# VectorE's order in the last phase: left to the scheduler, or written in the source with a pair's update spread over the next pair's evictions

## The chip, the cores and the metric

The kernel runs on one core of a Trainium2 chip. A core has five engines with queues of their own: TensorE (matmul), VectorE, ScalarE, GpSimd, and SyncE, which here issues DMAs. An instruction is issued in the order of its engine's queue, once the semaphores that it waits for have been counted up by the instructions it depends on. The metric is the device time of one launch in microseconds, lower is better.

## The reference

Two layers on 128 graphs of 128 nodes with 256 features, each wrapped in a residual and a layer norm. The first is a gated graph convolution. The second, which the change touches, joins a convolution branch and a message branch in a gated recurrent unit:

```python
# layer 0
norm = jnp.power(jnp.sum(adj, axis=-1) + 1e-06, -0.5)[..., None]
f_hom = jnp.einsum('bnm,bmd->bnd', adj, (x @ theta) * norm) * norm
gate = jax.nn.sigmoid(x @ W_t + b_t)
x = _layernorm(x + jax.nn.elu(gate * f_hom + (1.0 - gate) * (x @ W_h)))
# layer 1
h = jax.nn.relu(_bn(_conv1d(xc, conv1_w, 0), ...))
h = _bn(_conv1d(h, conv2_w, 8), ...)
x_conv = jnp.transpose(jax.nn.relu(h + xc), (0, 2, 1))
s = x @ w_se.T + b_se
A = jnp.exp(-dist(s)) * adj
x_nmp = jnp.einsum('bnm,bmd->bnd', A, jax.nn.relu(x @ w_msg.T + b_msg))
gi = jnp.concatenate([x_conv, x_nmp], axis=-1) @ w_ih.T + b_ih
gh = x @ w_hh.T + b_hh
r = jax.nn.sigmoid(gi_r + gh_r)
z = jax.nn.sigmoid(gi_z + gh_z)
nn_ = jnp.tanh(gi_n + r * gh_n)
x = _layernorm(x + (1.0 - z) * nn_ + z * x)
```

All of it is float32.

## The kernel before

The kernel has three phases. The first (to about 662 us) runs layer 0, `conv1` and the analysis of the 17-tap convolution into a frequency basis, two graphs at a time. The second multiplies in that basis, one pair of frequencies per step (L789 to L822), to about 839 us. The last phase, from 839 us to the end, takes the 128 graphs in 32 groups g of four, `NG` = 32, and each group in two pairs pr of two graphs.

In the last phase a group passes through these functions:

- `l1_own` (L945): masks the coordinates (`own`, VectorE L958), once per four groups after a transpose on TensorE and a copy on ScalarE (`turned`).
- `l1_kernel` (L963), for two groups at once: distance matmuls into `acc`, exponential on ScalarE (L976), times the adjacency on VectorE (`AT`, L980).
- `l1_project` (L921): sums of the node features on GpSimd (`sh`), message matmuls into two PSUM banks, evicted by VectorE with the bias (`msg`, L937), relu on ScalarE (L941). Groups 2 and 3 (`EARLY`) have their messages from an earlier phase.
- `l1_synth` (L890), for two groups at once: matmuls back from the frequency basis into `acc`, four evictions on VectorE (L914, with scale and residual), each with a relu on ScalarE (L917, `xcT`), then sums on GpSimd (`sc`).
- `l1_gather` (L983): messages times `AT` on TensorE, copied by ScalarE (`nmpT`, L993), then four sums on VectorE (`sm`, L1003 to L1006).
- `l1_gru` (L1041), per pair: the gate matmuls in seven products (Strassen's scheme with Winograd's sums). Each product is three float32 matmuls (of `sh`, `sc`, `sm` or the plain tiles, with the weights or the factors `t_h`, `t_c`, `t_m` that `l1_factors` makes once at the start, L844 to L847) into one PSUM bank. VectorE evicts each bank while adding it to a running sum: L1069 (product 0), L1072 (1), L1073 (5), L1074 (6), L1075 (4), L1096 (3), L1097 (2). GpSimd adds two more (L1094, L1095).
- `l1_update` (L1010), per pair: the elementwise end of the recurrent unit and the layer norm. It is a generator. Its steps are tanh of both gates on ScalarE (L1015), then on VectorE L1019, L1021 (with ScalarE's tanh L1022 behind), L1025, L1027, L1029, L1031, the statistics (L308, L309) with GpSimd's rstd (L192, L193), `nb` on VectorE (L316), the normalisation on ScalarE (L318) and the store of the result (L1038, SyncE's queue).

PSUM in this phase: four banks that go round (`psC`, taken through `bankc`), for messages, `nmp`, transposes and products; and one tile of four banks (`acc`), shared by the synthesis and the distance matmuls. `o` and `y` have two buffers each, `u1` to `p5` one.

The order. The code is issued through a scheduler that sorts each engine's instructions by priorities and its own view of times. Inside `tc.manual_schedule(engines=...)` the engines named keep the order of the source. Before, that held in the last phase for TensorE alone (L1104), and for TensorE, VectorE and ScalarE in the very last pair (L1133), whose update is written out by halves (L1076 to L1093). Everywhere else in the last phase VectorE's order was the scheduler's: a pair's update ran through at once in the source (L1098), and the scheduler put its steps between the next pair's evictions.

Of the kernel before, what the change touches and what calls it, by code (L numbers as in the profile page):

```python
# [18 lines left out]
G = 4  # L19
# [15 lines left out]
def gnn_layers_kernel(ctx: ExitStack, tc: tile.TileContext, a: dict, out: bass.AP):  # L35
# [80 lines left out]
    st = {}  # L116
# [206 lines left out]
    def nodes(q):  # L323
        return slice(q * P, (q + 1) * P)
# [246 lines left out]
    E = mybir.EngineType  # L571
# [218 lines left out]
    with tc.manual_schedule(engines={E.Activation, E.Pool}):  # L790
        for k in range(M // 2):
# [3 lines left out]
            y = yb.tile([P, 2, D], F32, tag="y", name=f"yb_{k}")  # L795
# [62 lines left out]
    def load_x1(g):  # L858
# [10 lines left out]
            s["x1"], x1_d[2 * g : 2 * g + 2].rearrange("r j n e -> n (r j) e")  # L869
        )  # L870

    sy = {}

    def load_y(d):
# [15 lines left out]
    def l1_synth(d):  # L890
        four = acc.tile([P, 4, 512], F32, tag="acc", name=f"conv2_ps_{d}")
        pcs = {}
        for e in range(2):
            for c in range(NC):
                pc = pcs[e, c] = four[:, NC * e + c, :]
                for q in range(G):
                    nc.tensor.matmul(  # L897
                        pc[:, nodes(q)], lhsT=sy[2 * d + e][0][:, q, c * P : (c + 1) * P], rhs=S,
                        start=(q == 0), stop=False, skip_group_check=True,
                    )  # L900
        for e in range(2):
            for c in range(NC):
                k = slice(32 * (NC * e + c), 32 * (NC * e + c) + 32)
                nc.tensor.matmul(  # L904
                    pcs[e, c], lhsT=sy[2 * d + e][1][k, :],
                    rhs=SLb[k].rearrange("p q n -> p (q n)"),
                    start=False, stop=True, skip_group_check=True,
                )
        for e in range(2):
            s = st[2 * d + e]  # L910
            s["xcT"] = ck.tile([P, NC, G * P], F32, tag="xcT", bufs=3, name=f"xcT_{2 * d + e}")
            for c in range(NC):
                dst = s["xcT"][:, c, :]
                nc.vector.scalar_tensor_tensor(  # L914
                    dst, pcs[e, c], scale2[:, c : c + 1], s["x1T"][:, c, :], ALU.mult, ALU.add
                )
                nc.scalar.activation(dst, dst, AF.Relu, bias=shift2[:, c : c + 1])  # L917
            l1_sums(2 * d + e, "c", s["xcT"], nc.gpsimd)


# [42 lines left out]
    def l1_kernel(*groups):  # L963

        pd = acc.tile([P, G, 512], F32, tag="acc", name=f"dist_ps_{groups[0]}")
        for i, g in enumerate(groups):
            turned, own = st[g]["turned"], st[g]["own"]
            for q in range(G):
                k = slice(q * P // G, (q + 1) * P // G)
                nc.tensor.matmul(  # L970
                    pd[:, q, i * P : (i + 1) * P], lhsT=turned[k, 0, :], rhs=own[k, :],
                    start=True, stop=True, skip_group_check=True,
                )
        for i, g in enumerate(groups):
            AT = st[g]["AT"] = ck.tile([P, G * P], F32, tag="AT", bufs=3, name=f"AT_{g}")
            nc.scalar.activation(  # L976
                AT.rearrange("p (q n) -> p q n", q=G), pd[:, :, i * P : (i + 1) * P],
                AF.Exp, scale=-1.0,
            )
            nc.vector.tensor_mul(AT, AT, st[g]["adjT"].rearrange("p q n -> p (q n)"))  # L980


    def l1_gather(g):  # L983
        s = st[g]
        nmpT = ck.tile([P, NC, G * P], F32, tag="nmpT", name=f"nmpT_{g}")
        for c in range(NC):
            pn = bankc(f"nmp_ps_{g}_{c}")
            for q in range(G):
                nc.tensor.matmul(  # L989
                    pn[:, nodes(q)], lhsT=s["msg"][:, q, c * P : (c + 1) * P],  # L990
                    rhs=s["AT"][:, nodes(q)], start=True, stop=True,
                )
            nc.scalar.activation(nmpT[:, c, :], pn, AF.Copy)  # L993
        l1_sums(g, "m", nmpT, nc.vector)


    def l1_sums(g, kind, src, engine):

        v = src.rearrange("p c (r j n) -> p c r j n", r=G // 2, j=2)
        a11, a12, a21, a22 = (v[:, c, :, j, :] for j in range(2) for c in range(NC))  # L1000
        t = ck.tile([P, 4, G // 2, P], F32, tag=f"s{kind}", name=f"s{kind}_{g}")
        s1, s2, s3, s4 = (t[:, i] for i in range(4))
        engine.tensor_tensor(s1, a21, a22, ALU.add)  # L1003
        engine.tensor_tensor(s2, s1, a11, ALU.subtract)
        engine.tensor_tensor(s3, a11, a21, ALU.subtract)
        engine.tensor_tensor(s4, a12, s2, ALU.subtract)  # L1006
        st[g][f"f{kind}"] = (a11, a12, s4, a22, s1, s2, s3)
# [33 lines left out]
    def l1_gru(g, pr, between=()):  # L1041

        s = st[g]
        y = ck.tile([P, 2, D], F32, tag="y", name=f"y_{g}_{pr}")
        add, sub = ALU.add, ALU.subtract

        made = iter(range(7))
        between = dict(between)

        def product(i):  # L1050
            k = next(made)
            if k in between:
                between[k]()
            pg = bankc(f"g_ps_{g}_{pr}_{i}")
            for k, (kind, lo) in enumerate((("h", 0), ("c", P), ("m", P))):
                nc.tensor.matmul(  # L1056
                    pg[:, lo : lo + 3 * P], lhsT=s[f"f{kind}"][i][:, pr, :], rhs=factors[kind][i],
                    start=(k == 0), stop=(k == 2), skip_group_check=True,
                )
            return pg  # L1060

        def sums(name):
            return ck.tile([P, 2 * D], F32, tag=name, bufs=1, name=f"{name}_{g}_{pr}")


        o = ck.tile([P, 2, 2, 2 * D], F32, tag="o", name=f"o_{g}_{pr}")
        u1, u2, u3, u4, p5 = (sums(q) for q in ("u1", "u2", "u3", "u4", "p5"))
        v = nc.vector
        v.tensor_tensor(u1, product(0), bias[:, 0, :], add)  # L1069
        final = g == NG - 1 and pr + 1 == G // 2  # L1070
        if not final:
            v.tensor_tensor(o[:, 0, 0, :], product(1), u1, add)  # L1072
        v.tensor_tensor(u2, product(5), u1, add)  # L1073
        v.tensor_tensor(u3, product(6), u2, add)  # L1074
        v.tensor_tensor(p5, product(4), bias[:, 1, :], add)  # L1075
        if final:  # L1076

            v.tensor_tensor(o[:, 1, 1, :], u3, p5, add)
            v.tensor_tensor(o[:, 1, 0, :], u3, product(3), sub)
            steps = [l1_update(g, pr, o[:, 1:2], y[:, 1:2], 1, 2)]  # L1080
            next(steps[0])
            v.tensor_tensor(u4, u2, p5, add)
            next(steps[0])
            next(steps[0])
            v.tensor_tensor(o[:, 0, 0, :], product(1), u1, add)
            next(steps[0])
            v.tensor_tensor(o[:, 0, 1, :], product(2), u4, add)
            steps.append(l1_update(g, pr, o[:, 0:1], y[:, 0:1], 0, 1))
            next(steps[1])
            for k in range(9):  # L1090
                for step in steps if k < 7 else reversed(steps):
                    next(step, None)
            return  # L1093
        nc.gpsimd.tensor_tensor(u4, u2, p5, add)  # L1094
        nc.gpsimd.tensor_tensor(o[:, 1, 1, :], u3, p5, add)  # L1095
        v.tensor_tensor(o[:, 1, 0, :], u3, product(3), sub)  # L1096
        v.tensor_tensor(o[:, 0, 1, :], product(2), u4, add)  # L1097
        for _ in l1_update(g, pr, o, y, 0, 2):  # L1098
            pass
        if pr + 1 == G // 2:  # L1100
            del st[g]

    ND = NG // 2
    with tc.manual_schedule(engines={mybir.EngineType.PE}):  # L1104
        load_c(0)
        load_c(1)
        load_y(0)
        for g in range(2):
            load_x1(g)
            l1_own(g)  # L1110
        l1_project(0)
        l1_kernel(0, 1)
        l1_project(1)
        l1_factors()
        l1_synth(0)
        for g in range(NG):
            d = g // 2
            if g + 2 < NG:
                load_c(g + 2)
                if g % 2 == 0:  # L1120
                    load_y(d + 1)
                load_x1(g + 2)
                l1_own(g + 2)
            l1_gather(g)
            if 2 <= g + 1 < NG:
                l1_project(g + 1)
            l1_gru(g, 0)
            if g % 2 == 1 and d + 1 < ND:
                l1_synth(d + 1)
            if g + 1 < NG:  # L1130

                l1_gru(g, 1, {4: lambda: l1_kernel(g + 1, g + 2)} if g % 2 == 1 else {})
    with tc.manual_schedule(engines={E.PE, E.DVE, E.Activation}):  # L1133
        l1_gru(NG - 1, 1)
    cctx.close()
# [41 lines left out]
```

## Time and profile before

| | us |
|---|---|
| median of three runs | 1980.65 (1980.35 to 1981.75) |
| the profiled execution | 1981.01 |
| its span, first to last instruction | 1979.2 |
| TensorE matmul busy | 1948.1 (98%) |
| VectorE busy | 1452.3 (73%) |
| ScalarE busy | 743.7 (38%) |
| GpSimd busy | 704.4 (36%) |

The costliest groups by line in the last phase are the products (L1056), with 44% of the chain that ended last. VectorE's groups in this phase, between 870 and 1950 us (busy us and mean ns of one, then idle time just before them and what ended it):

```profile
L1019 DVE SCALAR_TENSOR_TENSOR o<-o 128x512 f32<-128x512 f32 x63 | 52.8, 838 | 69.2 <-ACT o L1015 69.2
...
L1097 DVE TENSOR_TENSOR o<-g_ps,u 128x512 f32<-128x512 f32 x62 | 42.9, 692 | 81.9 <-PE g_ps L1056 81.9
...
L1005 DVE TENSOR_TENSOR sm<-nmpT 128x256 f32<-128x256 f32 x31 | 28.7, 927 | 0.0
L1003 DVE TENSOR_TENSOR sm<-nmpT 128x256 f32<-128x256 f32 x31 | 20.8, 671 | 0.0
...
L316 DVE SCALAR_TENSOR_TENSOR nb_b<-mv_b,rstd_b 128x2 f32<-128x2 f32 x62 | 17.8, 287 | 57.2 <-POOL rstd_b L193 57.2
```

How to read it: a timeline row is start, duration, engine, line, operation, output<-input, count, and in brackets the idle time before it and what released it. DVE is VectorE, ACT ScalarE, POOL GpSimd, PE TensorE, PEld TensorE's weight loads, SPq SyncE's queue. A row can join several instructions (x4). Successive rows of an engine may overlap by a little[...].

Two groups of the last phase take 70.4 us of TensorE: from one synthesis to the next, 1245.83 to 1316.18 in the chain of waits.

### The profile page before, as it was taken

What the parts mean: (1) busy time and instruction counts of PE and PEld (TensorE: products, weight loads), DVE (VectorE), ACT (ScalarE), POOL (GpSimd) and SP (SyncE); (2) the same over time, 40 slices, a digit from 0 to 9 for tenths busy, and PEclk for the clock granted to TensorE, in tenths of its full rate; (3) what the DMA queues carried; (4) which work ended last, traced back from release to release, by engine and by line L of the source; (5) the groups of instructions that cost most, each with busy time, mean ns of one, the idle gap of its engine ahead of it and who ended that gap; (6) DMA issues with size and microseconds to landing.
All of it is one profiled execution on the core that took longest, in us unless ns stands there. A gap on an engine that the chain in (4) does not pass through costs nothing.

```text
span 1979.2 us, 26038 instructions
## 1 busy us (share of the span) xinstructions
PE 1948.1 (98%) x8203; PEld 1323.2 (67%) x8203; DVE 1452.3 (73%) x2862; ACT 743.7 (38%) x1489; POOL 704.4 (36%) x987
## 2 busy tenths in 40 slices
PE   8999999999999999999999999999999999999996
PEld 5666666666666888866666666666666666666663
DVE  7888888888888644477667767677776776776775
ACT  3666666666666311122322222222232222222221
POOL 4232323222222355533424333333342433333331
PEclk9999999999999999999999999999999999999998
DMA  6787878777776899952212211221222222121100
GB/s 167 204 237 213 240 211 243 228 230 217 228 224 196 279 331 332 322 175 82 81 56 74 76 60 59 81 80 50 66 81 62 68 76 66 60 75 54 37 12 22
DMA packets 328687, 279.87 MB, mean 141 GB/s; under 512 B 150885, under 2 KB 268909, under 8 KB 328550
## 3 DMA queue, kind: packets, MB, share of 16 engines
q1 hardware_dynamic: 317622, 264.32, 43.4%
q0 software_dynamic: 4224, 8.37, 1.6%
q10 hardware_dynamic: 6704, 5.52, 0.9%
q8 instruction: 67, 1.10, 0.2%
q14 instruction: 70, 0.57, 0.1%
HBM read 173.26 MB, written 104.86 MB: 141 GB/s over the span
## 4 chain that ended last, share of the span: by engine, by line
PE 95%; DVE 2%; DMA 1%; issue 0%; ACT 0%; POOL 0%; SPq 0%; POOLq 0%; DVEq 0%; ACTq 0%
PE g_ps L1056 44%; PE f_ps L353 11%; PE y_ps L798 5%; PE msg_ps L933 5%; PE conv_ps L445 5%; PE gate_ps L358 5%; PE nmp_ps L989 3%; PE conv_ps L897 3%; PE coef_ps L466 3%; PE z_ps L811 3%; PE mix_ps L379 2%; PE w_ps L482 2%; PE conv_ps L904 1%; PE wl_ps L509 1%; PE adj_ps L333 1%; DMA x1b<-x_d 1%
## 5 line engine op out<-in xcount | busy, mean ns | idle before, releaser
L353 PE MATMUL f_ps<-w,xT 128*128 128x512 f32 x512 | 245.9, 603 | 2.4 <-DVE xT L423 1.4
L192 POOL TENSOR_SCALAR rstd_b<-mv_b 128x2 f32<-128x2 f32 (+1 forms) x65 | 12.5, 192 | 529.7 <-DVE mv_b L309 529.7
L1015 ACT ACTIVATE o<-o 128x1024 f32<-128x1024 f32 (+1 forms) x65 | 67.8, 1044 | 273.8 <-DVE o L1097 258.7
L353 PEld LDWEIGHTS f_ps<-w,xT 128*128 128x128 f32 x512 | 89.6, 190 | 103.5 <-issue 68.4
L1056 PE MATMUL g_ps<-t_h,sh 128*128 128x384 f32 x384 | 156.8, 490 | 0.0
L1056 PE MATMUL g_ps<-t_c,sc 128*128 128x384 f32 x384 | 155.2, 486 | 0.0
L1056 PE MATMUL g_ps<-t_m,sm 128*128 128x384 f32 x384 | 155.2, 486 | 0.0
L318 ACT ACTIVATE y<-y,nb_b,rstd_b 128x256 f32<-128x256 f32 x128 | 70.0, 593 | 212.4 <-DVE nb_b L316 212.4
L358 PEld LDWEIGHTS gate_ps<-w,xT 128*128 128x128 f32 x512 | 97.3, 190 | 68.1 <-issue 54.3
L1094 POOL TENSOR_TENSOR u<-u,p 128x512 f32<-128x512 f32 x63 | 79.8, 1267 | 162.2 <-DVE p L1075 162.2
L358 PE MATMUL gate_ps<-w,xT 128*128 128x256 f32 x512 | 131.4, 379 | 0.0
L798 PE MATMUL y_ps<-wb,H 128*128 128x256 f32 x544 | 128.3, 379 | 0.0
L806 POOL TENSOR_TENSOR ws<-wb 128x512 f32<-128x512 f32 x67 | 94.2, 1407 | 88.1 <-PE z_ps L811 59.5
L445 PE MATMUL conv_ps<-conv_w,x1T 128*128 128x259 f32 x512 | 122.6, 381 | 0.6 <-DVE x1T L423 0.6
L192 POOL TENSOR_SCALAR rstd_a<-mv_a 128x2 f32<-128x2 f32 x64 | 12.2, 191 | 288.7 <-DVE mv_a L309 222.4
L362 ACT ACTIVATE hom<-f_ps,norm 128x256 f32<-128x256 f32 x128 | 60.7, 474 | 142.8 <-PE f_ps L353 142.8
L798 PEld LDWEIGHTS y_ps<-wb,H 128*128 128x128 f32 x544 | 103.4, 190 | 14.0
L933 PE MATMUL msg_ps<-w_msg,cx1T 128*128 128x256 f32 x480 | 108.7, 379 | 0.0
L445 PEld LDWEIGHTS conv_ps<-conv_w,x1T 128*128 128x128 f32 x512 | 97.1, 190 | 16.0 <-PE w_ps L482 1.4
L1056 PEld LDWEIGHTS g_ps<-t_c,sc 128*128 128x128 f32 x384 | 73.0, 190 | 50.9
L1056 PEld LDWEIGHTS g_ps<-t_m,sm 128*128 128x128 f32 x384 | 73.0, 190 | 50.9
L1056 PE MATMUL g_ps<-w_hhT_w,cx1T 128*128 128x384 f32 x256 | 105.1, 492 | 0.0
(221 smaller groups left out, 4448.0 us busy)
## 6 DMA issues: line engine op xcount, KB each, us to landing
wb<-w_d SPq DMA_DIRECT2D x68, 512.0 KB
w_d<-w_o SPq DMA_DIRECT2D x32, 1024.0 KB
y_d<-yb SPq DMA_DIRECT2D x68, 256.0 KB
x<-in_x SPq DMA_DIRECT2D x64, 256.0 KB
x_d<-x SPq DMA_DIRECT2D x64, 256.0 KB
cx1T<-x1T_d SPq DMA_DIRECT2D x64, 256.0 KB
yt<-y_d SPq DMA_DIRECT2D x32, 512.0 KB
cx<-x_d SPq DMA_DIRECT2D x32, 512.0 KB
```

Of the source, the lines that this page charges most:

```text
L318: nc.scalar.activation(dst[:, q, :], src[:, q, :], AF.Identity, bias=nb[:, q : q + 1], scale=rstd[:, q : q + 1],)
L353: nc.tensor.matmul(pf, lhsT=xT[:, c, nodes(j)], rhs=w0[:, c, 0 : 2 * D], start=(c == 0), stop=(c == NC - 1),)
L358: nc.tensor.matmul(pg[:, j * D : (j + 1) * D], lhsT=xT[:, c, nodes(j)], rhs=w0[:, c, 2 * D : 3 * D], start=(c == 0), stop=(c == NC - 1),)
L362: nc.scalar.activation(hom[:, j, :], pf[:, 0:D], AF.Copy, scale=norm[:, j : j + 1])
L445: nc.tensor.matmul(ph[:, 0 : D + CO], lhsT=s["x1T"][:, c, nodes(j)], rhs=conv1_w[:, c, :], start=(c == 0), stop=(c == NC - 1),)
L466: nc.tensor.matmul(pa[:, c * M : (c + 1) * M], lhsT=h[:, j, c * P : (c + 1) * P], rhs=A, start=True, stop=True,)
L798: nc.tensor.matmul(py[:, blk, :], lhsT=coefs(blk if k == 0 else 2 * k + 1 - blk, c), rhs=w[:, blk, c, :], start=(c == 0), stop=(c == NC - 1),)
L806: nc.gpsimd.tensor_tensor(ws, w[:, 0], w[:, 1], ALU.add)
L933: nc.tensor.matmul(pm[:, j * D : (j + 1) * D], lhsT=x1T[:, c, nodes(q)], rhs=w_msg[:, c, :], start=(c == 0), stop=(c == NC - 1),)
L1015: nc.scalar.activation(rz, rz, AF.Tanh, scale=0.5)
L1056: nc.tensor.matmul(pg[:, lo : lo + 3 * P], lhsT=s[f"f{kind}"][i][:, pr, :], rhs=factors[kind][i], start=(k == 0), stop=(k == 2), skip_grou ...
L1094: nc.gpsimd.tensor_tensor(u4, u2, p5, add)
```

## The change

VectorE joins TensorE in the manual schedule of the last phase. A pair's update no longer runs through where it is made. It is put on a list, `pending`, and `fill(n)` takes up to n steps from it. The calls of `fill` stand between the next pair's evictions, in the synthesis, behind the exponential and in the gather.

```diff
+    pending = []
+
+    def fill(n):
+        for _ in range(n):
+            if pending and next(pending[0], pending) is pending:
+                pending.pop(0)
+
...
@@ l1_synth
+        fill(3)
         for e in range(2):
...
             for c in range(NC):
...
+            fill(1)
             l1_sums(2 * d + e, "c", s["xcT"], nc.gpsimd)
@@ l1_kernel
+            fill(1)
             nc.vector.tensor_mul(AT, AT, st[g]["adjT"].rearrange("p q n -> p (q n)"))
@@ l1_gather
             nc.scalar.activation(nmpT[:, c, :], pn, AF.Copy)
+        fill(2)
         l1_sums(g, "m", nmpT, nc.vector)
@@ l1_gru
         final = g == NG - 1 and pr + 1 == G // 2
+        fill(1)
         if not final:
             v.tensor_tensor(o[:, 0, 0, :], product(1), u1, add)
+            fill(1)
         v.tensor_tensor(u2, product(5), u1, add)
+        fill(2)
         v.tensor_tensor(u3, product(6), u2, add)
+        fill(2)
         v.tensor_tensor(p5, product(4), bias[:, 1, :], add)
+        fill(1)
...
         v.tensor_tensor(o[:, 1, 0, :], u3, product(3), sub)
+        fill(9)
         v.tensor_tensor(o[:, 0, 1, :], product(2), u4, add)
-        for _ in l1_update(g, pr, o, y, 0, 2):
-            pass
-        if pr + 1 == G // 2:
-            del st[g]
+        pending.append(l1_update(g, pr, o, y, 0, 2))
+        fill(1)
 
     ND = NG // 2
-    with tc.manual_schedule(engines={mybir.EngineType.PE}):
+    with tc.manual_schedule(engines={E.PE, E.DVE}):
...
                 l1_gru(g, 1, {4: lambda: l1_kernel(g + 1, g + 2)} if g % 2 == 1 else {})
+        fill(9)
     with tc.manual_schedule(engines={E.PE, E.DVE, E.Activation}):
         l1_gru(NG - 1, 1)
```

What the built program has of it. On VectorE the order of a typical pair is now: evict product 0, one update step, evict product 1, one step, product 5, two steps, product 6, two steps, product 4, the rest up to the norm, product 3, what is left, product 2. Between two groups the gate steps L1019 and L1021 stand ahead of the four `sm` steps, which are now together, and the `msg` evictions come right behind these. At the start of the phase the twelve factor subtractions, which the scheduler had put partly between the first `msg` evictions and the `AT` products, now stand in one block behind both groups' `msg` and `AT` and ahead of the first four `xcT` evictions. TensorE's order is unchanged. On GpSimd, the norm's rstd of an even group's first pair moves behind L1094 and L1095 of its second pair, and that of an odd group's first pair behind the four `sc` sums. On ScalarE, the normalisation of an odd group's first pair moves behind the relus of `xcT`. On SyncE, the two loads of a group's `x1T` stand together in every second group, where a result's store stood between them.

## The prediction

> **What bounds the kernel now.** I read the engine table and its slices first (TensorE 98% busy, the granted clock at nine tenths or more everywhere but in the last slice), then the last phase alone, by stretches:
>
> ```profile
> core 0: us, PE busy (x) PEld busy (x) DVE busy (x) ACT busy (x) POOL busy (x), PEclk, DMA share, GB/s
> ...
> 1500.00:1600.00 100.00, 100.00 (x410) 66.05 (x409) 69.77 (x130) 25.89 (x38) 36.19 (x44) 1.00 0.21 64
> ...
> 1900.00:1980.00 80.00, 60.33 (x209) 37.31 (x207) 49.91 (x102) 17.40 (x27) 18.10 (x25) 0.90 0.05 17
> ```
>
> See that TensorE is busy for 100.00 of 100 us with a granted clock of 1.00, while VectorE has 30% of its time free. TensorE's timeline has no gap from its first instruction of the phase (839.60, L949) to its last matmul (ends 1960.33), and the chain of waits is TensorE alone from 1232 to 1960. So VectorE's time is not paid for as such. It is paid for only where VectorE makes TensorE late, and after 1960.33. A TensorE instruction can wait for VectorE in three ways: its PSUM bank is not yet evicted (four banks in turn, so each `bankc` tile waits for the eviction of the fourth before it), an operand is not ready (`sm`, `xcT` through ScalarE, `own`, `AT`, `msg`, the factors `t_h`, `t_c`, `t_m`), or the four-bank `acc` tile is still being read.
>
> The tightest places before, from the timeline:
>
> ```profile
> 1484.42 0.68 DVE L937 TENSOR_TENSOR msg<-msg_ps,b_msg 128x512 f32<-128x512 f32 x1
> ...
> 1485.51 0.49 PE L1056 MATMUL g_ps<-t_h,sh 128*128 128x384 f32 x1
> ```
> ```profile
> 1537.95 1.40 DVE L914 SCALAR_TENSOR_TENSOR xcT<-conv_ps,scale,cx1T 128x512 f32<-128x512 f32 x2
> ...
> 1540.19 0.73 PE L970 MATMUL dist_ps<-own,turned 32*128 32x128 f32 x16
> ```
>
> The first bank of `msg_ps` is read out by 1485.10, and product 5, which takes that bank, starts at 1485.51: 0.4 us to spare. The last eviction of `conv_ps` ends at 1539.35, and the distance matmuls, which take `acc`, start at 1540.19: 0.8 us to spare. TensorE never waited, but nearly did.
>
> **The change part by part.** No instruction is added or removed: VectorE has 2854 before and after, TensorE's order is the same. What moves is VectorE's order in the last phase, and behind it a few instructions of GpSimd, ScalarE and SyncE.
>
> *Steady state.* Where TensorE has no gap nothing can be won, so only new waits count. I walked VectorE's new order through the two groups from 1474 to 1548 with the durations of the rows: 0.60 us from start to start for a 128x512 step, 0.73 where it reads the one just before it (L1019 at 1529.66, L1021 at 1530.39), and an eviction 0.2 us after TensorE's nominal end.
>
> - First pair of an even group: o's eviction (L1097) at 1476.45 and the two gate steps as before, then the four `sm` steps in a row (0.4 to 0.95 us each, with GpSimd's sums beside them), ending near 1483.2. The first `msg_ps` eviction follows at 1483.2 instead of 1484.4. Its bank is needed at 1485.51: margin 1.6 us instead of 0.4. `sm` is needed at 1486.80.
> - First pair of an odd group: here GpSimd takes u4 and o (1.27 us each, L1094 and L1095) ahead of the norm's rstd, and VectorE's `nb` (L316) waits for it. L1075 at 1505.1 starts them at 1505.85, they end at 1508.4, rstd takes 1 us, `nb` runs at 1509.4. Queued behind it on VectorE is L1097, which had run at 1509.00 and now runs at 1509.5; ScalarE's tanh and `nmpT` wait for that and for its norm step. Then `sm` ends near 1515.0 and `msg_ps` is read at 1515.7, needed at 1517.84: margin 2.1 us.
> - Synthesis: `fill(3)` puts three update steps ahead of the four `xcT` evictions and the update's last steps behind them. They would run from 1532.5 to about 1535.9 instead of 1535.43 to 1539.35, so `acc` is free 4.3 us before the distance matmuls. Product 0's bank is read at 1537.2, needed at 1540.85.
> - The other `nb` waits (1.1 us each; L316's row has 57.2 us of waiting over 62) stand in front of L1074 or L1075, whose banks are wanted 3 us or more later.
>
> Sum 0, hidden by TensorE. If the 1.6 us cover were missed by 0.5 us, 28 of the 32 groups (those that project `msg` here) would pay it each: 14 us. SyncE's queue: the two halves of `cx1T` now go before an output store and not around it. Those loads were issued at 1435.16 and 1437.09 for matmuls at 1510.52, so 0. Freed later is `x1`, by about 1 us at L1031 (SyncE's L868 waits for it), and its load is wanted some 60 us later: 0.
>
> *The start of the phase.* Here VectorE was behind. Before, the first five factor subtractions ran in its waits for `msg_ps` and for ScalarE's exponential; now all twelve come after both groups' `msg` and `AT`.
>
> ```profile
> 851.42 0.56 DVE L847 TENSOR_TENSOR t_m<-t_m,w_ihT_w 128x384 f32<-128x384 f32 x1
> ...
> 852.59 2.73 DVE L914 SCALAR_TENSOR_TENSOR xcT<-conv_ps,scale,cx1T 128x512 f32<-128x512 f32 x4 [0.42 <-PE conv_ps L904]
> 853.38 0.72 ACT L917 ACTIVATE xcT<-xcT,shift 128x512 f32<-128x512 f32 x1 [2.85 <-DVE xcT L914]
> ...
> 854.91 0.49 PE L1056 MATMUL g_ps<-w_ihT_w,xcT 128*128 128x384 f32 x1
> ...
> 858.04 0.83 DVE L1004 TENSOR_TENSOR sm<-sm,nmpT 128x256 f32<-128x256 f32 x1
> ...
> 859.42 0.81 PE L1056 MATMUL g_ps<-t_m,sm 128*128 128x384 f32 x2
> ```
>
> See that VectorE had waited 0.42 us for `conv_ps` before L914. In the new order: `own` to 841.81, the first `msg` evictions at 841.81 and 843.53, `AT` when the exponentials end (845.8 and 846.3) at 845.9 and 846.5, group 1's `msg` at 847.1 and, TensorE's end at 847.80 setting it, 847.83, done at 848.43. Then the twelve. Successive subtractions stand 0.467 us apart (844.14, 844.61, 845.08). Of the new sequence three (L845 directly behind L844, for each kind) read what the one just before wrote.
>
> Here a rule bears. The Trainium skill's "VectorE: DVE Perf Modes", section "The DRAIN you can't avoid", says that the next instruction waits for the pipe to empty anyway, so that a semaphore between chained ones costs nothing extra. The row says otherwise: L1021 behind L1019 came 0.73 us later where independent ones of that size come at 0.60, so 0.12 more. By the rule the block takes 12 x 0.467 = 5.6 us and L914 starts at 854.03, 1.44 late; by the row 9 x 0.467 + 3 x 0.59 = 5.97, at 854.40, 1.81 late. I take the row.
>
> ScalarE's first relu ended at 854.10; product 0's second matmul started at 854.91. With 0.06 us from ScalarE's end to TensorE's start (L816's end 839.54, L949 at 839.60) the cover was 0.75, so TensorE waits 1.81 - 0.75 = 1.06 us. Next, `sm`'s second step ended at 858.87 for a matmul at 859.42: cover 0.49. It too moves by 1.81 (its start hangs on ScalarE's `nmpT`, behind the relus), 1.32 in all, of which 1.06 is paid: 0.26 more. GpSimd's sums for product 5 had 1.7 us to spare, and the banks 1 us or more after this shift. **Start: 1.32 us** (0.95 by the rule). Bounds: 0 if `AT` and the factors run closer than I have them, 2.5 if every subtraction takes 0.1 us more.
>
> *The end.* The final pair is written out as before, but (31, 0)'s norm steps land differently: the second statistics step now stands behind L1078 (0.6 us), so `nb` moves from 1957.81 to 1958.43, while L1082 goes ahead of it and fills the wait. ScalarE's two norm steps (1.09 us) then end at 1959.7 and hold the half-pair's tanh (L1022) from 1959.41 to 1959.70. L1025 follows at 1960.18 and L1087 at 1960.52 instead of 1960.37. **End: 0.15 us**, bounds -0.4 to +0.6 (VectorE's wait of 0.53 for rstd gone; or the whole 0.62 of `nb` passed on).
>
> Sum: +1.47 us. On the profiled execution, span 1979.2 becomes 1980.7 and its time 1981.01 becomes 1982.5. That execution lies 0.36 above the median of the runs; against the median 1980.65 I forecast **1982.1 us**.
>
> **Rivals.**
> 1. *Hidden start*: `AT` and the factor block run tighter and the 0.75 and 0.49 us cover most. For it: only 1 us is at stake. Against: twelve subtractions cannot go in less than 5.6 us. Time 1980.9.
> 2. *Slower, by VectorE's order in the steady state*: strict order lets one late `nb` or `sm` hold the evictions behind it, and product 5 waits for the `msg_ps` bank. The Trainium skill's "Perfetto Trace Analysis", in "Tensor Engine Instruction (MATMUL, LD_WEIGHTS)", calls VectorE, ScalarE and GpSimd strict FIFOs, so nothing can overtake; the scheduler's order was as strict, but was made from its own view of times. It decides once the first `msg_ps` eviction is later than my walk by 1.6 us in even groups or 2.1 in odd. At 0.5 us past this, 28 x 0.5 + 1.5 = 15.5 us: 1996. For it: L1003 and L1005 swing between 0.41 and 0.95 us when GpSimd works beside them. Against: the old order had only 0.4 us and never paid.
> 3. *Faster*: the only TensorE gap (0.47 us at 839.1, on ScalarE) and the 18.9 us behind 1960.33 are all there is to win. The first is not touched; VectorE's wait at L316 before the end (0.53) could go: 1980.1. Over 0.2% would need 4 us off the end, for which nothing speaks.
> 4. *It doesn't do what it says*: the interleave stands in the built order, so only its worth is in doubt; this is the forecast itself.
>
> **How the numbers follow.** Forecast (start and end cost 0.7 to 3 us) 0.67; hidden 0.14; slower by the steady state 0.16; faster 0.03. A measurement here tells about 0.2%, 4 us, from no change. Forecast, hidden and nearly all of rival 3's time lie inside it; rival 2 lies outside. So faster 0.02, same 0.82, slower 0.16. Range: below to rival 3's edge and the runs' own spread, 1980.3; above 1986, where the steady state would lose 0.13 us a group. The likeliest case alone gives 1981.3 to 1983.7.
>
> **What would show it.** Right: TensorE stays at 100.00 in every stretch from 900 to 1900; a wait of TensorE for ScalarE's `xcT` of about 1 us near 855 and a small one for `sm` near 860; L914 in the steady state ahead of the old place by some 3 us; L316's waits as large as before; last matmul near 1961.7. Wrong: TensorE waiting for L937 or L914 once per group or per two groups, or a start of the phase without a gap.

## The result, and the profile after

The changed kernel takes **1984.61 us** (median of 15 runs, 1983.87 to 1985.88), against 1980.89 for the kernel before on the same chip: a ratio of 1.0020, with an interval of 1.0013 to 1.0028. Forecast were 1982.1 and a range of 1980.3 to 1986.0. So the time lies in the range and just inside what was called no change, but the loss is 3.7 us where 1.5 was forecast. The profiled execution has a span of 1982.3 us where the one before had 1979.2, 3.1 more; the rest of the 3.7 lies within the spread of the runs.

To find the 3.1 us, divide the span at TensorE. The last phase is counted here from its first transpose to the end of its last matmul, because the place where it begins (838 to 841 us in all the runs below) moves with the earlier phases.

| | phase starts | phase | behind it | span |
|---|---|---|---|---|
| before | 839.60 | 1120.73 | 18.90 | 1979.2 |
| after | 839.27 | 1123.81 | 19.24 | 1982.3 |
| difference | -0.33 | +3.08 | +0.34 | +3.1 |

First the stretches of the changed kernel (columns: stretch, its length, then busy time of TensorE, its weight loads, VectorE, ScalarE, GpSimd; then granted clock, DMA share, GB/s):

```profile
870.00:890.00 20.00, 19.20 (x71) 11.82 (x70) 14.20 (x28) 5.25 (x8) 6.21 (x8) 1.00 0.21 66
890.00:1000.00 110.00, 110.00 (x462) 71.17 (x461) 82.33 (x150) 29.42 (x45) 44.63 (x52) 1.00 0.24 74
1000.00:1900.00 900.00, 900.00 (x3692) 587.77 (x3691) 644.18 (x1175) 242.72 (x365) 345.00 (x408) 1.00 0.21 65
1900.00:1940.00 40.00, 39.66 (x149) 25.54 (x149) 28.02 (x52) 10.12 (x15) 14.50 (x17) 1.00 0.04 14
```

From 890 to 1900 TensorE is busy for every microsecond, as before, at a granted clock of 1.00. The steady state lost nothing. The loss sits at the two ends of the phase: 870 to 890 lacks 0.80 us, 1900 to 1940 lacks 0.34. TensorE's timeline shows three waits after the phase's first instruction, the rows with brackets (the row at 858.46, and ScalarE's row ahead of it, are for later):

```profile
855.66 0.91 PE L1067 MATMUL g_ps<-w_ihT_w,xcT 128*128 128x384 f32 x2 [0.92 <-ACT xcT L925]
...
857.83 0.58 ACT L1003 ACTIVATE nmpT<-nmp_ps 128x512 f32<-128x512 f32 x1
...
858.46 0.91 PE L1067 MATMUL g_ps<-w_ihT_w,nmpT 128*128 128x384 f32 x2
...
886.47 0.91 PE L1067 MATMUL g_ps<-w_ihT_w,nmpT 128*128 128x384 f32 x2 [0.80 <-ACT nmpT L1003]
...
1937.01 0.91 PE L1067 MATMUL g_ps<-w_ihT_w,nmpT 128*128 128x384 f32 x2 [0.34 <-ACT nmpT L1003]
```

The first was forecast, for `xcT`. The two for `nmpT` were not: they lie in groups 1 and 31. A wait costs more than its bracket, about 0.26 here: the bracket counts from the modelled end of the matmul before, though in a dense row the next one starts 0.16 ahead of that end (pairs of 0.81 us start every 0.645), and the pair behind the wait takes 0.91 instead of 0.81. So the two for `nmpT` come to 1.06 and 0.60, and the first to 1.18. How much each place costs is settled below, by taking them away: 1.41 at the start of the phase, 1.06 in group 1 and 0.60 in group 31, together 3.07.

**What happens in groups 1 and 31.** These are rows of VectorE, GpSimd and ScalarE ahead of the wait in group 1, in the changed kernel:

```profile
879.60 1.26 POOL L1110 TENSOR_TENSOR u<-u,p 128x512 f32<-128x512 f32 x1 [11.12 <-DVE p L1090]
...
880.35 0.18 DVE L309 BATCH_NORM_AGGREGATE mv_b<-stats_b 128x2 f32<-128x6 f32 x1
...
880.82 1.26 POOL L1111 TENSOR_TENSOR o<-u,p 128x512 f32<-128x512 f32 x1
...
882.17 0.19 POOL L192 TENSOR_SCALAR rstd_b<-mv_b 128x2 f32<-128x2 f32 x1
...
882.44 0.71 POOL L193 TENSOR_TENSOR rstd_b<-rstd_b,neg_half 128x2 f32<-128x2 f32 x1
...
883.12 0.72 POOL L1014 TENSOR_TENSOR sh<-cx1T 128x256 f32<-128x256 f32 x1
883.18 0.68 DVE L316 SCALAR_TENSOR_TENSOR nb_b<-mv_b,rstd_b 128x2 f32<-128x2 f32 x1 [1.80 <-POOL rstd_b L193]
883.79 0.68 DVE L1114 TENSOR_TENSOR o<-g_ps,u 128x512 f32<-128x512 f32 x1
...
883.90 1.09 ACT L318 ACTIVATE y<-y,nb_b,rstd_b 128x256 f32<-128x256 f32 x2 [8.99 <-DVE nb_b L316]
...
884.90 1.04 ACT L1026 ACTIVATE o<-o 128x1024 f32<-128x1024 f32 x1
...
885.84 1.05 ACT L1003 ACTIVATE nmpT<-nmp_ps 128x512 f32<-128x512 f32 x2
```

Read it from the bottom. `nmpT` stands third in ScalarE's queue: behind the norm's two steps (L318, 1.09 us) and behind the tanh of the next pair (L1026, 1.04). The tanh hangs on product 2's eviction (L1114), which stands behind `nb` (L316) on VectorE. L318 begins only at 883.90 because `nb` has waited 1.80 us for `rstd`. And `rstd` came late because the statistics of this pair (done at 880.53) were spread to behind product 4: that eviction releases u4 and o on GpSimd (L1110, L1111, 1.26 us each), and `rstd` (L192) stands behind these in its queue. Before, ScalarE had done the norm 2.6 us ahead of the tanh, while TensorE was at products 4 and 3. This is the timeline of the kernel before in group 31:

```profile
1928.43 0.16 DVE L316 SCALAR_TENSOR_TENSOR nb_b<-mv_b,rstd_b 128x2 f32<-128x2 f32 x1 [1.11 <-POOL rstd_b L193]
...
1928.68 1.09 ACT L318 ACTIVATE y<-y,nb_b,rstd_b 128x256 f32<-128x256 f32 x2 [6.21 <-DVE nb_b L316]
...
1932.35 1.06 ACT L1015 ACTIVATE o<-o 128x1024 f32<-128x1024 f32 x1 [2.58 <-DVE o L1097]
...
1933.31 1.07 ACT L993 ACTIVATE nmpT<-nmp_ps 128x512 f32<-128x512 f32 x2
```

The same late `nb` occurs at every step from an even group to an odd one (ahead of an even group `nb` does not wait behind u4 and o). In most of them TensorE projects `msg` (3.4 us of matmuls) between `nmp_ps` and product 0, and `nmpT` may be late. Two odd groups have nothing to project at that place: group 1, because the group after it (2) is one of the two whose `msg` comes from the DMA, and group 31, because none comes after it. There product 0 follows `nmp_ps` directly.

Why do the two pay differently, 0.80 and 0.34 us of waiting? In group 1 `nb` itself takes 0.68 us and ends 0.02 behind the end of GpSimd's sum L1014; in group 31, where there is no next group to sum for, GpSimd does nothing at that moment and `nb` takes 0.16 (at 1934.20). `nmpT` follows TensorE's start of `nmp_ps` by 3.41 us in the one and by 2.96 in the other. The last section has more on such steps.

### The profile page after: what moved, and what is told of

The parts are those of the page before. It is cut to its first block, busy times and chain, and to the rows that moved or that the text cites. A ratio compares the mean times of both kernels' runs of the same rounds, so it can differ in the third digit from the quotient of the medians.

```text
span 1982.3 us, 25995 instructions
## 1 busy us (share of the span) xinstructions
PE 1950.9 (98%) x8203; PEld 1323.4 (67%) x8203; DVE 1453.9 (73%) x2862; ACT 740.7 (37%) x1489; POOL 716.0 (36%) x987
## 4 chain that ended last, share of the span: by engine, by line
PE 94%; DVE 3%; DMA 1%; ACT 1%; POOL 1%; issue 1%; SPq 0%; POOLq 0%; DVEq 0%; ACTq 0%
PE g_ps L1067 42%; PE f_ps L353 11%; PE y_ps L798 5%; PE conv_ps L445 5%; PE gate_ps L358 5%; PE msg_ps L942 5%; PE coef_ps L466 3%; PE conv_ps L904 3%; PE z_ps L811 3%; PE nmp_ps L999 3%; PE mix_ps L379 3%; PE w_ps L482 2%; PE wl_ps L509 1%; PE conv_ps L911 1%; PE adj_ps L333 1%
## 5 line engine op out<-in xcount | busy, mean ns | idle before, releaser
L318 ACT ACTIVATE y<-y,nb_b,rstd_b 128x256 f32<-128x256 f32 x128 | 70.0, 593 | 438.0 <-DVE nb_b L316 438.0
L1110 POOL TENSOR_TENSOR u<-u,p 128x512 f32<-128x512 f32 x63 | 79.9, 1268 | 249.6 <-DVE p L1090 249.6
L192 POOL TENSOR_SCALAR rstd_b<-mv_b 128x2 f32<-128x2 f32 (+1 forms) x65 | 12.9, 198 | 342.6 <-DVE mv_b L309 341.2
L1026 ACT ACTIVATE o<-o 128x1024 f32<-128x1024 f32 (+1 forms) x65 | 67.6, 1040 | 138.6 <-DVE o L1114 129.5
L192 POOL TENSOR_SCALAR rstd_a<-mv_a 128x2 f32<-128x2 f32 x64 | 12.2, 191 | 289.8 <-DVE mv_a L309 223.5
```

The source lines that it names most:

```text
L318: nc.scalar.activation(dst[:, q, :], src[:, q, :], AF.Identity, bias=nb[:, q : q + 1], scale=rstd[:, q : q + 1],)
L1026: nc.scalar.activation(rz, rz, AF.Tanh, scale=0.5)
```

## The experiments

Each was to take away one of the suspected places, or to press on one until it gives. The time is quoted beside the phase of the profiled execution, since differences of 1 us are within the spread of the runs but not of the phase: kernels below that lose the same agree in it within 0.01. The kernel before took 1980.90 us beside these runs, and 1980.09 on the chip on which the norm was put behind `nmpT`.

### The first subtractions of the factors back to their old place

```diff
-    def l1_factors():
+    def l1_factors(kinds):
...
         l1_project(0)
+        l1_factors("h")
         l1_kernel(0, 1)
         l1_project(1)
-        l1_factors()
+        l1_factors("cm")
```

> The four t_h subtractions go back between group 0's messages and the exponentials; the other eight stay where the change put them. If the start of the phase is what the factor block costs: L922's first eviction (854.11 in the changed kernel, 14.84 us after the phase starts) comes at about 13.0 to 13.3, TensorE's wait for xcT near 855.66 (0.92 us) is gone, and product 5's first matmul comes about 1.3 us earlier; the waits near 886 (0.80) and 1937 (0.34) stay; time about 1.3 us under the changed kernel, near 1983.3 on the scale of its median 1984.61. If strict order costs a little everywhere: TensorE still has a wait near 855 or one of the same size later, and the time stays within 0.3 us of the changed kernel.

Measured: 1982.17 us, the phase 1122.46, so **1.35 us less**. VectorE's timeline in this kernel:

```profile
842.56 0.69 DVE L947 TENSOR_TENSOR msg<-msg_ps,b_msg 128x512 f32<-128x512 f32 x1 [1.03 <-PE msg_ps L943]
843.16 0.55 DVE L845 TENSOR_TENSOR t_h<-w_hhT_w 128x384 f32<-128x384 f32 x1
843.75 0.56 DVE L846 TENSOR_TENSOR t_h<-w_hhT_w,t_h 128x384 f32<-128x384 f32 x1
844.22 0.55 DVE L847 TENSOR_TENSOR t_h<-w_hhT_w 128x384 f32<-128x384 f32 x1
844.69 0.55 DVE L848 TENSOR_TENSOR t_h<-t_h,w_hhT_w 128x384 f32<-128x384 f32 x1
845.16 1.29 DVE L991 TENSOR_TENSOR AT<-AT,cadjT 128x512 f32<-128x512 f32 x2
...
851.62 2.73 DVE L923 SCALAR_TENSOR_TENSOR xcT<-conv_ps,scale,cx1T 128x512 f32<-128x512 f32 x4
```

The four subtractions fill the time in which VectorE waits for the exponentials. The `xcT` evictions start at 851.62, 12.99 us after the phase's start as in the kernel before (12.99) and not 14.84. TensorE's wait at 855 is gone; those for `nmpT` stay at 0.81 and 0.34. The small delay at 858.46 is gone with it. The start of the phase is a cost of its own and of this size.

### `nb` behind the eviction, alone

```diff
         v.tensor_tensor(o[:, 1, 0, :], u3, product(3), sub)
-        fill(9)
         v.tensor_tensor(o[:, 0, 1, :], product(2), u4, add)
+        fill(9)
```

> The last fill of a pair goes behind product 2's eviction, so nb (L316), which waits 1.8 us for rstd in an even group's second pair, no longer stands ahead of that eviction. If VectorE's queue alone (nb ahead of the eviction) makes nmpT late: both TensorE waits, near 886 (0.80) and 1937 (0.34), are gone, about 1.7 us with what follows them. If it is ScalarE's queue (the two norm steps, 1.09 us, still ahead of nmpT): product 2's eviction and the tanh come about 1 us earlier, but nmpT only 0.2 to 0.4 us earlier, because the norm steps now stand between the tanh and nmpT; the wait near 886 shrinks to 0.4 to 0.6, the one near 1937 to 0 to 0.2; together 0.4 to 0.7 us.

Measured: 1983.65 us, the phase 1123.46, **0.35 less**; both waits are still there, 0.39 and 0.39 us. ScalarE's timeline:

```profile
882.19 1.06 ACT L1026 ACTIVATE o<-o 128x1024 f32<-128x1024 f32 x1 [8.58 <-DVE o L1113]
883.16 1.08 ACT L318 ACTIVATE y<-y,nb_b,rstd_b 128x256 f32<-128x256 f32 x2
884.14 1.06 ACT L1003 ACTIVATE nmpT<-nmp_ps 128x512 f32<-128x512 f32 x2
```

This phase starts 1.30 us earlier than the changed kernel's, so on that kernel's clock the tanh came at 883.49 instead of 884.90, 1.41 earlier, and `nmpT` at 885.44 instead of 885.84, only 0.40 earlier. The obvious reading, that `nb` blocks the eviction behind it on VectorE, is not enough: the norm has only changed places with the tanh, and both still stand ahead of `nmpT`. In group 31 nothing came of it, where 0 to 0.2 us of the wait was expected to be left: it was 0.34 and is 0.39. With the order tanh, norm, `nmpT` the start of the norm no longer matters, and both groups wait the same.

### `nb` and the norm behind `nmpT`

```diff
-        fill(9)
         v.tensor_tensor(o[:, 0, 1, :], product(2), u4, add)
         pending.append(l1_update(g, pr, o, y, 0, 2))
-        fill(1)
+        next(pending[-1])
...
-        fill(2)
+        fill(len(pending) + 1)
         l1_sums(g, "m", nmpT, nc.vector)
```

> nb goes behind product 2's eviction and the own step, and the norm's two ScalarE steps behind both nmpT evictions; nothing else changes place. Moving nb alone behind the eviction (the earlier run) left waits of 0.39 and 0.39 us, with the norm still ahead of nmpT. If those 1.09 us of ScalarE are what is left: the tanh at about 883.6, nmpT at 884.6 instead of 885.84 on the changed kernel's clock, no wait of TensorE near 886 and 1937, the phase 1122.1 to 1122.2, as with the early statistics. If the eviction itself still comes too late for other reasons (u4 and o of GpSimd): waits of about 0.4 stay.

Measured: 1982.41 us, the phase 1122.14, **1.67 less**, and no wait for `nmpT` anywhere:

```profile
884.07 1.06 ACT L1026 ACTIVATE o<-o 128x1024 f32<-128x1024 f32 x1 [8.58 <-DVE o L1113]
885.03 1.06 ACT L1003 ACTIVATE nmpT<-nmp_ps 128x512 f32<-128x512 f32 x2
885.98 1.08 ACT L318 ACTIVATE y<-y,nb_b,rstd_b 128x256 f32<-128x256 f32 x2
```

`nmpT` starts at 884.45 on the changed kernel's clock (this phase starts 0.58 later). What was left of the waits in the run before was ScalarE's 1.09 us. (The norm alone behind `nmpT`, with `nb` left ahead of the eviction, was not run.)

### The statistics one step earlier

```diff
         v.tensor_tensor(u3, product(6), u2, add)
-        fill(2)
+        fill(3)
```

> Three steps instead of two behind product 6's eviction: the statistics of an even group's first pair come before product 4's eviction, and GpSimd takes rstd ahead of u4 and o. nb then runs near 881 instead of 883.2, the norm's two ScalarE steps near 881.1, and nmpT follows the tanh at about 884.6 instead of 885.84. If late statistics are the cause: no wait of TensorE near 886 and 1937, no new one elsewhere, the phase about 1.7 us shorter than the changed kernel's (the wait near 855.66 stays), the time about 1982.9 on the scale of 1984.61. If the order is not the cause: the waits stay, or as much appears in other groups.

Measured: 1982.31 us, the phase 1122.15, **1.66 less**; of the three waits only the one for `xcT` is left (0.93). The norm starts 1.3 us later than expected (883.95, or 882.42 on the changed kernel's clock, where 881.1 was expected): `nb` came as early as expected (882.69, or 881.16) but took 1.22 us, beside GpSimd's L1110 (882.63 to 883.89). It still starts before the tanh, and `nmpT` at 886.17, which is 884.64. So the same 1.66 us is recovered from either end of the chain: statistics early enough, or norm late enough.

### Both edits

The first and the fourth together.

> The t_h subtractions ahead of the exponentials and the statistics ahead of product 4's eviction, together. One at a time they took 1.35 and 1.66 us off the last phase (1123.81 to 1122.46 and 1122.15; phase counted from its first transpose to its last matmul's end). If the three TensorE waits are all that the change costs before the end: no wait of TensorE in the phase, its length 1120.7 to 1120.9 (before 1120.73), TensorE busy for all of every stretch, and what is left against the kernel before is the 0.35 us behind the last matmul. If the strict order costs something more that the traces do not show as a wait: the phase stays above 1121.2.

Measured: 1981.09 us against 1980.90 for the kernel before (ratio 1.0002, 0.9994 to 1.0011), and the phase 1120.74 where that one has 1120.73. No wait of TensorE is left. Compared group by group with the changed kernel, by the start of `nmp_ps`, this kernel is 1.40 us ahead from group 1 and 2.46 from group 2, stays at 2.46 to 2.47 through group 31, and ends 3.07 ahead. So the three places cost 1.41, 1.06 and 0.60, and **strict order itself costs nothing** in the 29 groups between. Nor does the order of SyncE's loads and stores, which these edits leave as the change made it.

### The end by hand

The last lines of the phase, on top of both edits: (31, 0)'s update is taken step by step behind the last pair's evictions (`fill(9)` in front of the last block goes, a `fill(1)` stands ahead of its product 0), its `nb` behind the half pair's second gate step, and so its norm behind the half pair's second tanh; and the first half's `nb` stands three steps later. Product 6 is followed by two steps in this pair, as in the changed kernel.

```diff
+            fill(9)
             v.tensor_tensor(o[:, 0, 0, :], product(1), u1, add)
...
-            for k in range(9):
-                for step in steps if k < 7 else reversed(steps):
-                    next(step, None)
+            a, b = steps
+            for step in (a, b, a, b, a, b, a, b, b, b, a, b, b):
+                next(step, None)
```

> As the run with both edits, and the end written out: the first pair's update of the last group is spread by hand over the last pair (statistics ahead of the half pair's evictions, nb and the norm behind the half pair's second tanh), and the first half's nb stands behind three more steps of the second half. If the 0.35 us of the end is the late statistics and the norm ahead of the half pair's tanh, it goes; and if nb's wait of 0.71 us for rstd ahead of the second half's L1040 is on the path, another 0.7: 18.1 to 18.3 us from the last matmul's end to the end of the span, against 19.22 in the changed kernel and 18.87 in the one before; the time 0.3 to 0.7 us under the kernel before, which only the trace can show. If the end hangs on something else (the store's own time), it stays at 18.8 to 19.2.

Measured: 1980.57 us against 1980.90 (ratio 0.9996, 0.9988 to 1.0004), the phase 1120.73, and behind it 18.16 us, 1.08 under the changed kernel and 0.74 under the one before (the expectation's 19.22 and 18.87 are from rounded spans). Of the 1.08, 0.34 stands at the last eviction: it starts 0.04 us behind the last matmul's end, as before the change (0.04), where the changed kernel has 0.38. The other 0.74 comes behind it. The timeline of VectorE, first the changed kernel, then this one, at the first half's `nb`:

```profile
1968.43 0.16 DVE L316 SCALAR_TENSOR_TENSOR nb_b<-mv_b,rstd_b 128x1 f32<-128x1 f32 x1 [0.71 <-POOL rstd_b L193]
1968.50 0.42 DVE L1040 SCALAR_TENSOR_TENSOR o<-o 128x256 f32<-128x256 f32 x1
```
```profile
1965.39 0.39 DVE L1039 SCALAR_TENSOR_TENSOR o<-o 128x256 f32<-128x256 f32 x1
1965.82 0.42 DVE L1041 SCALAR_TENSOR_TENSOR o<-o 128x256 f32<-128x256 f32 x1
1966.28 0.42 DVE L1043 TENSOR_TENSOR y<-o,cx 128x256 f32<-128x256 f32 x1
1966.69 0.16 DVE L316 SCALAR_TENSOR_TENSOR nb_b<-mv_b,rstd_b 128x1 f32<-128x1 f32 x1
```

The 0.71 us wait is gone because useful steps cover it. The time cannot tell this kernel from the one before (0.3 us, with intervals that hold 1); only the trace shows the gain.

### How near its edge the steady state is

Extra VectorE steps ahead of each group's first message eviction:

```diff
         msg = ck.tile([P, G, D], F32, tag="msg", name=f"msg_{g}")
+        if g > 1:
+            pad = ck.tile([P, 2 * D], F32, tag="pad", bufs=1, name=f"pad_{g}")
+            for _ in range(2):
+                nc.vector.tensor_tensor(pad, bias[:, 0, :], bias[:, 1, :], ALU.add)
```

> Two extra VectorE steps of 128x512 (0.60 us each, 1.2 in all), whose result nothing uses, ahead of the first message eviction of each of the 28 groups that project messages here. If the walked margins hold (1.7 us in even groups, 2.2 in odd, read from the changed kernel's trace): no new wait of TensorE, the phase within 0.3 us of 1123.81. If the steady state is nearer its edge than that: TensorE waits for L950 once in most groups.

> Five such steps, 3.0 us. By the margins TensorE then waits 1.3 us in each of the 14 even groups and 0.8 us in each of the 14 odd ones for the message bank, ahead of product 5: 29 us in all, the time near 2013. If something else gives first (sm, whose steps come ahead of the padding, can't; own, the update's later steps or product 0 can): waits at another line, or a sum well off 29.

Measured with two steps: 1986.58 us, the phase 1126.25, **2.44 more** than the changed kernel, and no new wait is printed: it is spread in stalls too short for the view. Against the changed kernel, by the start of `nmp_ps`, each of groups 4, 8, 12, ... 28 loses 0.26 to 0.31 us, each of 6, 10, ... 26 loses 0.03 to 0.07, group 30 loses 0.27, and the odd ones 0.01 at most. The margin of 1.7 us that was read in one even group is not that of all. In group 16 of the changed kernel, VectorE's and TensorE's timelines have:

```profile
1415.35 1.27 DVE L946 TENSOR_TENSOR msg<-msg_ps,b_msg 128x512 f32<-128x512 f32 x2
...
1417.08 0.81 PE L1067 MATMUL g_ps<-t_h,sh 128*128 128x384 f32 x2
```

The first of the two evictions ends 0.67 later, at 1416.02, so 1.06 us before its bank is taken. That is the tightest; groups 4, 8, 12, 20, 24, 28 and 30 have 1.23 to 1.29. In group 18 and its like, which turn (the `turn_ps` transposes give VectorE 0.22 us more), the same lines give 1.51, and 2.03 in the odd group 19. The two steps took 1.32 us, a little more than the margin. In group 8 of the padded kernel they put the eviction's end to 1135.29, TensorE's product 5, due at 1135.25, starts at 1135.44, and its first pair takes 0.88 us instead of 0.81: together the 0.26.

Measured with five: 2050.30 us, the phase 1188.45, **64.6 more** where 29 was expected. The mechanism is the expected one: all the waits beside the three old ones are at product 5, for `msg_ps`, in the 28 groups. The sizes: the five steps took 3.50 us (0.70 each, as each writes the tile of the one before), not 3.0; TensorE waits 1.46 us in each of the 14 odd groups and 2.08 to 2.32 in each of the 14 even ones, some 51 in all; each wait costs 0.24 more than its bracket, 7 in all; and the remaining 7 us are four places where the clock fell, taken up in the last section.

### No spreading

VectorE's order still fixed in the source, but without the interleave:

```diff
-        pending.append(l1_update(g, pr, o, y, 0, 2))
-        fill(1)
+        for _ in l1_update(g, pr, o, y, 0, 2):
+            pass
```

> VectorE's order stays fixed in the source, but a pair's update runs through at once behind its own last eviction, as the source before the change has it. The chain from that eviction to nb is about 8.5 us by the rows of the changed kernel (tanh 1.04, two gates 1.4, tanh 0.63, four steps 2.8, statistics 1.2, rstd 1.0, hand-overs), and the next pair's first eviction waits behind all of it, where its bank is wanted 5.8 us after TensorE has filled it. If spreading the update is what keeps the steady state free: TensorE waits 1 to 2 us a pair, some 60 to 130 us in all, and the stretches from 1000 to 1900 show it busy for 90 to 97 of 100. If the evictions have more room than that: no wait, time within 3 us of the changed kernel.

Measured: **2192.11 us** (ratio to before 1.106, 1.104 to 1.108), 208 more than the changed kernel. TensorE's waits in this phase (waiting instruction, awaited one: us in all, times, longest), beside one of 0.9 for `xcT`:

```profile
PE g_ps L1067 <- DVE msg L946: 103.4, 28, 4.6
PE g_ps L1067 <- DVE u L1080: 38.0, 16, 2.4
PE g_ps L1067 <- DVE sm L1015: 12.2, 3, 5.2
```

They are for a message eviction, for product 0's and for `sm`, 154 us together. Most of the rest is the clock, which fell to 0.50 with many of these waits (last section): half of the time at 0.50 in which TensorE did not wait is 45 us. The guess of 60 to 130 us was too small, as it had neither waits of this length nor the clock. What the source of the kernel before said was thus never what ran: there the scheduler did the spreading, and with the order fixed the source must do it. The comparison with "before" is one of two interleaved orders, not of interleaved against plain.

## Why the prediction was right, and where its sum was short

- **Steady state 0: right in what it covered.** 890 to 1900 is at 100%, and the run with both edits has the old phase to 0.01 us. But the step that stands in the prediction as "Sum 0, hidden by TensorE" failed for two groups. It walked an odd group with messages, found `nb`, L1097 (now L1114) and ScalarE's norm late, and hid them behind a margin of 2.1 us that exists only where `msg` is projected after `nmp_ps`. It even named "28 of the 32 groups (those that project `msg` here)", and did not walk the others. Groups 1 and 31 pay 1.06 + 0.60 us. This 1.66, with 0.09 more at the start and 0.19 more at the end, less the 0.33 by which this execution began the phase earlier, is the shortfall of 1.6 us (3.1 measured against 1.47). The missed term is larger than any that was forecast; that the sum still fell into the range owes something to luck.
- **Within that step, the cause.** `nb` did come late as walked, but took 0.68 us where the walk gave it 0.1; the prediction listed "its norm step" among what waits. The runs showed that it reaches `nmpT` on two ways at once, by the eviction behind it on VectorE and by the norm's 1.09 us ahead of `nmpT` on ScalarE: moving `nb` behind the eviction gave 0.35 us, moving the norm behind `nmpT` as well 1.67. The second way alone was not run; by the rows the tanh could then not start before the eviction's end at 884.47 in group 1, so an estimate is that about half of that wait would stay.
- **Start 1.32 us: measured 1.41**, by the forecast mechanism for the greater part. L922 was put 1.81 us later by the spacing of the rows and 1.44 by the rule of the Trainium skill's "VectorE: DVE Perf Modes", "The DRAIN you can't avoid"; it came 1.85 later (14.84 after the phase's start instead of 12.99). Undoing a third of the block gave back 1.35. The wait for `xcT` cost 1.18 (0.92 in its bracket) where 1.06 was forecast: TensorE started 1.08 later, and the pair behind took 0.10 more, for which the sum had no term. What is left, 0.22, is not printed as a wait. It stands at 858.46, at the second half of `nmpT`, which ScalarE finishes at 858.41; the prediction had not asked when this operand would come. The 0.26 forecast for `sm` was not paid: `sm`'s second step ended at 860.24 for a matmul at 860.50. That the two sizes are alike is luck.
- **End 0.15 us: measured 0.34**, inside its bounds of -0.4 to +0.6. `nb` of (31, 0) runs 1.59 us before the last matmul's end where it ran 2.52 before it; the forecast had 0.62 of this. Of the 0.93, 0.34 reached the last eviction, and with it the end.
- **The walked margins of `msg_ps`**, 1.6 and 2.1 us, were right for the two groups that were walked (1.51 and 2.03), and too large for the other even groups (1.06 to 1.29). The rival by the steady state, which "decides once the first `msg_ps` eviction is later than my walk by 1.6 us in even groups", would have decided from 1.1 to 1.3; the run with 1.32 us of padding pays 2.4 us.
- **"L316's waits as large as before" was wrong**: 73.6 us over 65 instead of 59.4 over 65. Nearly all of it is hidden. (VectorE's count, too, is 2862 in the page before and after, not 2854.)
- **Rivals.** The hidden start falls: it was paid. Slower by the steady state falls, as the run with both edits shows. Faster falls: nothing of the 18.9 us at the end was won. As for the fourth, the interleave is in the timeline as written, and what it does is to stand in for the scheduler's.

## What to carry to other kernels

Hidden costs must be checked in every kind of group, and the odd kinds first: the first, the last, and those in which a piece of work that serves as cover is missing. Where a step stands late, list all queues that it passes through and not only the one it was moved on; here most of the price was paid through ScalarE's queue, in which nothing had been edited by hand. When an order is fixed in the source, the interleave that a scheduler had found must be written too: without it this phase loses over 200 us, with it 0.

## What the runs showed of the hardware that was not expected

**A stall of TensorE can cost its clock for some microseconds.** With five padding steps, TensorE's matmuls after one of the stalls, and the granted clock there (the number that follows GpSimd's busy time), were:

```profile
999.14 1.62 PE L1071 MATMUL g_ps<-t_h,sh 128*128 128x384 f32 x2 [2.29 <-DVE msg L950]
1000.55 1.49 PE L1071 MATMUL g_ps<-t_c,sc 128*128 128x384 f32 x2
1001.83 1.08 PE L1071 MATMUL g_ps<-t_m,sm 128*128 128x384 f32 x2
```
```profile
999.00:1001.00 2.00, 1.86 (x3) 1.18 (x4) 2.00 (x4) 1.06 (x1) 0.00 (x0) 0.50 0.03 8
1001.00:1003.00 2.00, 2.00 (x5) 1.06 (x4) 1.04 (x3) 0.00 (x0) 0.00 (x0) 0.66 0.00 0
1003.00:1006.00 3.00, 3.00 (x11) 1.74 (x10) 2.93 (x6) 0.00 (x0) 0.00 (x0) 1.00 0.00 0
```

A pair that takes 0.81 us takes 1.62 and 1.49, at a granted clock of 0.50, and the full clock is back after 3.4 us. This followed 4 of the 14 stalls of 2.1 to 2.3 us (in groups 4, 12, 18 and 24) and none of the 14 of 1.46; these groups lost 1.6 to 1.7 us more than the other even ones of their kind, half of the 3.4. The run without spreading has the longer stalls: there the clock fell with 1 of 16 of 2.35 to 2.38 us, 7 of 14 of 2.9 to 3.1, and all 17 of 3.3 to 5.2. The changed kernel, whose longest wait in this phase is 0.92, shows 1.00 from 870 to 1940. The Trainium skill's "TensorE: Matmul & The Clock Gate", in "HAM oscillation — how this bites in real kernels", warns of idle gaps over some 3.4 us. Here gaps of 2.1 to 3.1 us sufficed at times, 12 of 44 of them, and the measurement decides. What picks out the ones among stalls of the same length stays open.

**A short VectorE step can last as long as the GpSimd instruction beside it.** `nb`, 128x2 numbers, takes 0.16 us in the 50 of 65 cases of the changed kernel in which GpSimd runs nothing beside it, and 0.68 in the other 15, those in which one of the sums `sh` began just before it. All traces but that of the run without spreading have 15 or 16 such cases, with GpSimd's sums or its u4 beside them, of 0.22 to 1.23 us, and every one ends 0.01 to 0.02 us behind the end of the GpSimd instruction.

**Successive VectorE steps on the same tile stand further apart** than independent ones: 0.59 us against 0.47 for 128x384 (843.16, 843.75, 844.22 above), and 0.70 against 0.60 for the padding, where each step only overwrites what the one before wrote.
